# Softmax denominators from spare value columns, keys through DRAM, and one store for eight strips in a four-layer image kernel

## The chip, the core and the metric

The kernel runs on one core of one Trainium2 chip. Its time is the device time of one execution in microseconds; the figure quoted is the median of three runs. In the text PE is TensorE (PEld its weight loads), DVE is VectorE, ACT is ScalarE, POOL is GpSimd and SP is SyncE, which here only issues DMAs.

## The reference, cut to what matters

The input x is 4 images of 16 channels and 512 x 512 pixels. Four layers follow each other.

```python
# layer 0: window attention and MLP (C = 16, 2 heads of 8, windows of 8 x 8 pixels, hidden 64)
x = x + depthwise3x3(x) + pos_b                     # "position"
win = windows(affine(x))                            # 4*64*64 windows of T = 64 tokens
q, k, v = split(win @ qkv_w.T + qkv_b); q = q * 8**-0.5
out = softmax(q @ k.T) @ v                          # per window and head
x = x + out @ proj_w.T + proj_b
x = x + gelu(affine(x) @ fc1_w.T + fc1_b) @ fc2_w.T + fc2_b
# layer 1: fake-quantised 3x3 convolution; mean and variance over the WHOLE image batch; clip to 0..6
# layer 2: conv3x3, relu, conv3x3, + x        layer 3: conv3x3, 1x1 to 128, relu, 1x1 to 16, + x
```

Two facts matter below. The division by the softmax denominator may be done after the product with v. And layer 1 needs the largest |x| and the statistics of its convolution over everything before it can normalise, so the result of layer 0 goes to DRAM (`x1`) and is read back twice.

## The kernel before, in words

All arithmetic is float32 on PE except the quantised convolution of layer 1. There are three stages.

**Layer 0** (`window_attention`) takes 64 steps. The image is cut into 8 horizontal strips of 64 rows; a step does 8 rows and 64 columns of all 8 strips and 4 images at once. Partitions of `y` hold (4 pairs of strips `vv`) x (2 strips of a pair `w`) x 16 channels, its free dimension the 4 images `u` and 512 pixels. Attention wants another order, images on the partition quadrants and window tokens block-diagonal over the two strips; this is the tile `y2`, and `turn_keys` fills it for the next step by 32 small DMAs from `y`, eight at k = 1, 3, 5 and 7.

The order of the work on PE, DVE, ACT and SP is the order in which the source issues it (`manual_schedule`). A step does, for k = 0..7 (one pair of strips, four of its windows):

- `values(k)`: four PE transposes of `y2` into bank 4 or 6, and one DVE copy to `yt`;
- `scores(k)`: 16 matmuls `g` x `y2` into banks 0-3 (the tiles `pair`), then two ACT exponentials of 1024 columns each to `e`. There is one set of these banks, so scores(k+1) waits for both exponentials of k;
- `attend(e, yt, k)`: 16 matmuls of 128 columns, contracting over all 128 partitions (two strips x 64 tokens), give the unnormalised outputs in bank 4 or 6 (line L374); four matmuls of 512 columns with the constant `own` (the right half of tile `hot`) give the denominators, spread over the 16 channels, in bank 5 or 7 (L379);
- `divide(k)`: ACT takes Ln and Exp(-x) of the denominators (L388, L389), DVE multiplies (L390) into `o`.

In the loop scores runs one k ahead of attend and divide. The end of a step does `queries` of the next step (L324, banks 0-3), `project` (L398) with the residual added by DVE (L403), and then a mixed stage in which 16 `hidden` blocks (L411, gelu on ACT L416) are interleaved with the `depthwise` matmuls (L291) of step n + 2. The `output` of a step (fc2, L422, residual L427) is issued at the start of the next step, and every second step `store` writes 8 rows and 128 columns to `x1`: 16 DMAs of 32 KB for each image. The inputs come in by one 2.6 MB load for every two steps (`load`).

Each matmul is recorded twice[...].

**Statistics stage** (start of `conv_layers`): all of `x1` is read in 129 groups of two rows by `_load_pairs`, two DMAs of 256 KB each, into whatever tiles are free; POOL rounds, ACT converts, PE convolves and DVE takes the statistics.

**Layers 1 to 3** (rest of `conv_layers`): 128 iterations; `_load_pairs` reads `x1` a second time (tile `tx`), and between the convolutions SBUF-to-SBUF DMAs shift rows (`zo<-ze`, `ho<-he`, `xo<-xe`, `qo<-qe`).

## Time and profile before

| | us |
|---|---|
| median of 3 runs (6023.52 to 6040.93) | 6026.44 |
| the profiled execution: its time | 6030.1 |
| the profiled execution: its span | 6028.3 |
| of the span: set-up, to the first step | 63.4 |
| layer 0, 64 steps, to 3450 | 3386.6 |
| statistics stage, to 3775 | 325.0 |
| layers 1 to 3, to the end | 2253.3 |

The stage bounds were read off the timeline. A step of layer 0 repeats after 52.67 to 52.70 us in most cases. In the profile's lines "L355 PE MATMUL pair<-g,y 32*128 32x128 f32 x32" means line 355, engine, operation, output tile <- input tiles, the part of the PE array (rows * columns) that one instruction takes, the shape of its moving operand, and how many records are merged. "[1.13 <-ACT e L363]" is the idle time before it and what ended that. In the row of slices each digit is the busy share of one fortieth of the span, in tenths.

### The profile page before, as it was taken

Reading aid. Unit: us, or ns where it says so; the run is one execution under the profiler, and the core shown is the slowest. Engines: PE = TensorE matmul, PEld = TensorE weight load, DVE = VectorE, ACT = ScalarE, POOL = GpSimd, SP = SyncE. Lnnn points to the kernel's source line nnn. Section 1 sums busy time; section 2 is a strip of 40 time slices with the busy share of each in tenths; the row PEclk is TensorE's granted clock in tenths of the full one; section 3 lists DMA queues with packets and bytes.
Section 4 is the critical chain, followed back from the end, with each engine's and each line's share of the span. In section 5 each row is a group of like instructions: output and inputs, shape, how many; then the busy total and the mean of one; then the engine's idle time right before and its main releaser. Section 6 shows DMA issues by size and latency. Waiting matters only on the chain. (4 is left out here: it accounts for less than half of the span.)

```text
span 6028.3 us, 242228 instructions
## 1 busy us (share of the span) xinstructions
PE 5775.3 (96%) x108624; PEld 3084.9 (51%) x108624; DVE 3268.4 (54%) x4648; ACT 3837.6 (64%) x5257; POOL 171.1 (3%) x193
## 2 busy tenths in 40 slices
PE   8999999999999999999999866899999999999999
PEld 5666666666666666666666433333333333333333
DVE  3444444444444444444444455566666666666666
ACT  4777877877787777778777654344444444444444
POOL 0000000000000000000000154000000000000000
PEclk9999999999999999999999999999999999999999
DMA  3233333323333232333333398666676666666663
GB/s 84 58 71 66 64 77 62 78 59 71 67 64 77 61 79 59 71 66 65 77 61 61 58 243 216 163 171 168 167 173 165 168 172 166 168 171 168 167 170 104
DMA packets 638119, 674.57 MB, mean 112 GB/s; under 512 B 371728, under 2 KB 500880, under 8 KB 632976
## 3 DMA queue, kind: packets, MB, share of 16 engines
q1 hardware_dynamic: 635760, 657.53, 47.1%
q8 instruction: 857, 14.04, 1.0%
q0 software_dynamic: 1024, 1.05, 0.1%
q14 instruction: 190, 1.56, 0.1%
q10 hardware_dynamic: 288, 0.39, 0.0%
HBM read 221.15 MB, written 134.48 MB: 59 GB/s over the span
## 5 line engine op out<-in xcount | busy, mean ns | idle before, releaser
L363 ACT ACTIVATE e<-pair 128x1024 f32<-128x1024 f32 x1024 | 992.5, 1021 | 381.7 <-PE pair L355 381.7
L1175 ACT ACTIVATE hid<-tb,vec 128x512 f32<-128x512 f32 x1024 | 620.7, 688 | 517.5 <-PE tb L1167 517.4
L291 PE MATMUL pair<-x,taps 32*32 32x512 f32 x18432 | 927.4, 605 | 2.6 <-ACT y L302 1.2
L1177 DVE TENSOR_SCALAR hid<-tb,vec 128x512 f32<-128x512 f32 x1024 | 695.7, 742 | 2.7 <-PE tb L1167 2.6
L411 PE MATMUL bank<-y,fc_e 32*32 32x512 f32 x8192 | 680.1, 598 | 0.9 <-DVE y L403 0.9
L355 PE MATMUL pair<-g,y 32*128 32x128 f32 x16384 | 653.0, 285 | 26.9 <-ACT y L302 25.0
L355 PEld LDWEIGHTS pair<-g,y 32*128 32x128 f32 x16384 | 542.8, 186 | 215.9 <-issue 108.9
L416 ACT ACTIVATE hid<-bank,f1b 128x512 f32<-128x512 f32 x1024 | 644.5, 686 | 12.4 <-PE bank L411 4.8
L291 PEld LDWEIGHTS pair<-x,taps 32*32 32x32 f32 x18432 | 602.2, 103 | 98.2 <-issue 19.0
L347 DVE COPY yt<-bank 128x512 f32<-128x512 f32 x512 | 347.3, 688 | 540.2 <-PE bank L342 531.9
L1167 PE MATMUL tb<-ye,mat 32*128 32x512 f32 x4096 | 637.6, 624 | 0.3 <-DVE hid L1177 0.3
L374 PE MATMUL bank<-e,yt 128*32 128x128 f32 x16384 | 556.7, 276 | 3.4 <-issue 2.4
L390 DVE TENSOR_TENSOR o<-bank,r 128x512 f32<-128x512 f32 x512 | 354.2, 692 | 372.6 <-ACT r L389 356.3
L379 PE MATMUL bank<-e,hot 128*32 128x512 f32 x4096 | 535.6, 593 | 0.0
L1187 PE MATMUL tb<-hid,mat 128*32 128x512 f32 x4096 | 466.0, 595 | 41.6 <-DVE hid L1177 41.6
L374 PEld LDWEIGHTS bank<-e,yt 128*32 128x32 f32 x16384 | 418.0, 109 | 111.7 <-DVE yt L347 52.8
L306 DVE TENSOR_SCALAR y<-pair,vec 128x512 f32<-128x512 f32 x128 | 90.3, 746 | 706.5 <-PE pair L291 706.5
L1167 PEld LDWEIGHTS tb<-ye,mat 32*128 32x128 f32 x4096 | 267.0, 183 | 323.3 <-issue 219.9
L342 PEld LDWEIGHTS bank<-mat,y 128*128 128x128 f32 x2048 | 216.3, 141 | 376.1 <-issue 270.0
L1092 PE MATMUL tb<-zo,cw 64*32 64x512 f32 x3096 | 362.8, 594 | 14.9 <-issue 8.9
L1092 PE MATMUL tb<-xo,cw 64*32 64x512 f32 x3096 | 366.1, 600 | 10.1 <-issue 7.0
L1092 PE MATMUL tb<-xe,cw 64*32 64x512 f32 x3072 | 361.5, 600 | 0.0
(176 smaller groups left out, 7564.1 us busy)
## 6 DMA issues: line engine op xcount, KB each, us to landing
x<-in_xw_dram SPq DMA_DIRECT2D x32, 2600.0 KB, 10.9
zo<-ze SPq DMA_DIRECT2D x512, 128.5 KB, 2.4
ho<-he SPq DMA_DIRECT2D x512, 128.5 KB, 2.4
xo<-xe SPq DMA_DIRECT2D x512, 128.5 KB, 2.4
y<-y SPq DMA_DIRECT2D x2048, 32.0 KB, 2.2
tx<-x SPq DMA_DIRECT2D x256, 256.0 KB, 4.6
out_dram<-xe SPq DMA_DIRECT2D x128, 512.0 KB, 3.5
x<-xo SPq DMA_DIRECT2D x2016, 32.0 KB, 1.7
```

Source lines behind the costliest of these rows:

```text
L291: nc.tensor.matmul(bank(u)[quad(vv)], taps[quad(u), tap, :], xts[n // 2][quad(u), vv, dy : dy + WS, at : at + BW], start=tap == 0, stop=ta ...
L355: nc.tensor.matmul(bank(u)[:, P * jj : P * jj + P], y2[quad(u), vv, jl + jj].rearrange("p w t -> p (w t)"), g[quad(u), vv, jl + jj].rearra ...
L363: nc.scalar.activation(e[:, 2 * i : 2 * i + 2].rearrange("p u j t -> p u (j t)"), pairs[i], AF.Exp,)
L374: nc.tensor.matmul(b[quad(u), P * jj : P * jj + P], yt[:, jj, quad(u)], e[:, u, jj, :], start=True, stop=True,)
L379: nc.tensor.matmul(d[quad(u)], own, e[:, u].rearrange("p j t -> p (j t)"), start=True, stop=True,)
L411: nc.tensor.matmul(b[quad(k)], fc1[quad(vv), quad(k)], y[quad(vv), u, :], start=True, stop=True,)
L416: nc.scalar.activation(hd, b, AF.Gelu, bias=f1b)
L1092: nc.tensor.matmul(p[r][_quad(2 * f + w)], weights[_half(r), odd, dx, :], src[_half(r), f, dx : dx + W], start=dx == 0, stop=dx == 2,)
L1167: nc.tensor.matmul(p[q], w1[_quad(q), 1 - par, :], inner(src)[_quad(q), f, :], start=True, stop=True,)
L1175: nc.scalar.activation(hd, p[q], AF.Relu, bias=v("l3_b1"))
L1177: nc.vector.tensor_scalar(hd, p[q], v("l3_b1"), 0.0, ALU.add, ALU.max)
L1187: nc.tensor.matmul(p[r][_quad(c)], w2[:, par], hd, start=(r, c) not in seen, stop=(r, c) in seen,)
```

## The change

Layer 0:

- `values` adds a constant `other` instead of copying: the transposed values of a strip have zeros in the 16 columns of the other strip, and these get ones. `attend` then contracts each strip by itself over 64 partitions, so that its 16 output channels and, 16 times over, its denominator come from one matmul of 128 columns. The four matmuls with `own` are gone.
- `empty` copies the two banks to SBUF (`o`, `ts`); `gather` brings one row of denominators of each strip and image to the tile `sums` by two DMAs for each two k; `merge` brings the second strip's outputs from `ts` to their place in `o` by four DMAs.
- One step later, `invert` takes Ln and Exp of `sums` once (two ACT instructions of 1024 columns), and `divide` spreads the inverses by a DVE `stream_shuffle` and multiplies on POOL. Projection, hidden, output and store of a step move one step later, and a 65th pass of the loop finishes the last step. Half of the output moves into the mixed stage.
- `turn_keys` goes through DRAM: `put_keys` writes `y` to `yd` by four DMAs, and eight DMAs read it into `y2` after the step's last scores.
- The input is loaded for each step by itself (1.3 MB), two steps ahead.
- `x1` is laid out as (row pair m in a strip, row r of the pair, strip s, channel, image, column), so that `store` writes all eight strips with one DMA for each r; `_load_pairs` reads this layout.

```diff
-    x1 = dram.tile([H // 2 + 1, 2 * C, B, W], F32, name="x1")
+    x1 = dram.tile([SM, 2, NS + 1, C, B, W], F32, name="x1")     # SM = H // 16
...
+    yd = dram.tile([2, U, 32, V, N], F32, name="yd")
+    sums = [pa.tile([P, 1024], F32, name=f"sums{i}") for i in range(2)]
...
+    def put_keys(n):
+        for u in range(U):
+            nc.sync.dma_start(yd[n % 2, u].rearrange("q v x -> v q x"), ys[n][:, u])
+    def turn_keys(n, i):
+        u, w = divmod(i, 2)
+        at = slice(32 * u + C * w, 32 * u + C * w + C)
+        nc.sync.dma_start(
+            y2[at, :, :, w, :].rearrange("p v j t -> p (v j) t"),
+            yd[n % 2, u, C * w : C * w + C].rearrange("c v (j t) -> c (v j) t", t=T),
+        )
...
-        nc.vector.tensor_copy(t.rearrange("p j c -> p (j c)"), b)
+        nc.vector.tensor_tensor(t..., b..., other.unsqueeze(1).to_broadcast([P, 4 * U, 32]), ALU.add)
...
-        e = px.tile([P, U, 4, P], F32, tag="e", name=f"e{n}_{k}", bufs=3)
+        e = px.tile([P, U, 4, P], F32, tag="e", name=f"e{n}_{k}", bufs=2)
...
     def attend(e, yt, k):
-        b, d = bank(4 + 2 * (k % 2)), bank(5 + 2 * (k % 2))
+        p = bank(4 + 2 * (k % 2)), bank(5 + 2 * (k % 2))
         for jj in range(4):
             for u in range(U):
-                nc.tensor.matmul(
-                    b[quad(u), P * jj : P * jj + P], yt[:, jj, quad(u)], e[:, u, jj, :], ...)
+                for w in range(2):
+                    half = slice(64 * w, 64 * w + 64)
+                    nc.tensor.matmul(
+                        p[w][quad(u), P * jj : P * jj + P],
+                        yt[half, jj, quad(u)], e[half, u, jj, :], ...)
+    def empty(o, k, n):
+        vv, i = divmod(k, 2)
+        if i == 0:
+            ts[vv] = px.tile([P, 1024], F32, tag="t", name=f"t{n}_{vv}")      # 2 buffers
+        nc.vector.tensor_copy(part(o, k), bank(4 + 2 * i))
+        copy = nc.scalar.copy if i else nc.vector.tensor_copy
+        copy(ts[vv][:, 512 * i : 512 * i + 512], bank(5 + 2 * i))
+    def gather(o, vv, n):
+        d = sums[n % 2]
+        nc.sync.dma_start(d[2 * vv : P : 32], pair(o, vv)[C:P:32])
+        nc.sync.dma_start(d[2 * vv + 1 : P : 32], ts[vv][0:P:32])
+    def merge(o, vv):
         for u in range(U):
-            nc.tensor.matmul(d[quad(u)], own, e[:, u].rearrange("p j t -> p (j t)"), ...)
-        nc.scalar.activation(r, d, AF.Ln)
-        nc.scalar.activation(r, r, AF.Exp, scale=-1.0)
-        nc.vector.tensor_tensor(o[:, vv, jl : jl + 4]..., b, r, ALU.mult)
+            at = slice(32 * u + C, 32 * u + 2 * C)
+            nc.sync.dma_start(pair(o, vv)[at], ts[vv][at])
+    def invert(n):
+        d = sums[n % 2]
+        nc.scalar.activation(d, d, AF.Ln)
+        nc.scalar.activation(d, d, AF.Exp, scale=-1.0)
+    def divide(o, k, n):
+        r = px.tile([P, 512], F32, tag="r", name=f"r{n}_{k}")
+        vv, i = divmod(k, 2)
+        nc.vector.stream_shuffle(r, sums[n % 2][:, 512 * i : 512 * i + 512], [2 * vv] * C + [2 * vv + 1] * C)
+        nc.gpsimd.tensor_tensor(part(o, k), part(o, k), r, ALU.mult)
...
# store: one DMA for each r (two where the rows reach into the next strip), partitions = (strip, channel)
+                (next(queues) if k == STEPS // 2 - 1 else nc.sync).dma_start(
+                    x1[mm : mm + rows, r, s : s + 2 * V, :, u, XW * cb : XW * cb + XW].rearrange(
+                        "m s c x -> (s c) m x"),
+                    src[:, at : at + rows])
...
-    for n in range(STEPS):
+    for n in range(STEPS + 1):           # old = the o of step n - 1; done = n - 1
...
         if last:
             output(*last)
+        if old is not None:
+            invert(n - 1)
+            divide(old, 0, n - 1)
         for k in range(1, 8):
...
+                empty(o, k - 1, n)
+                if k % 2 == 0:
+                    gather(o, k // 2 - 1, n)
+                elif k > 1:
+                    merge(o, k // 2 - 1)
+            if old is not None:
+                divide(old, k, n - 1)
# after the loop: queries 0; attend 7, empty 7, gather 3; queries 1, turn_keys(n + 1), merge 3; project(old)
...
-        last = (y, xo, hids, range(U), (5, 7, 4, 6), n)
+                if q == 9:               # in the mixed stage
+                    output(y, xo, hids[:8], (0, 1), (6, 7), done)
+            put_keys(n + 2)
+        if loads:
+            xts[loads] = load(loads)
+        last = (y, xo, hids[8:], (2, 3), (5, 7), done) if old is not None else None
...
 def _load_pairs(nc, t, x1, tt):
+    s, m = divmod(2 * tt, SM)
...
-            t[64 * a : 64 * a + 32 * k],
-            x1[2 * tt : 2 * tt + k, :, 2 * a : 2 * a + 2].rearrange("m c f x -> (m c) f x"),
+            t[64 * a : 64 * a + 32 * k].rearrange("p f x -> p (f x)"),
+            x1[m : m + k, :, s, :, 2 * a : 2 * a + 2].rearrange("m r c f x -> (m r) c (f x)"),
```

## The prediction

> **What bounds the kernel now.** First the page's slices: PE is busy nine tenths everywhere except in slices 24 to 26, and there it is the DMA row that stands at 9 and 8.

> ```profile
> PE   8999999999999999999999866899999999999999
> ...
> DMA  3233333323333232333333398666676666666663
> GB/s 84 58 71 66 64 77 62 78 59 71 67 64 77 61 79 59 71 66 65 77 61 61 58 243 216 163 171 168 167 173 165 168 172 166 168 171 168 167 170 104
> ```

> So layer 0 and layers 1 to 3 are PE's, and the statistics stage is the DMA engines'. Next the timeline of one k in the middle of layer 0:

> ```profile
> 1503.17 1.17 PE L355 MATMUL pair<-g,y 32*128 32x128 f32 x32
> 1504.27 1.08 PE L374 MATMUL bank<-e,yt 128*32 128x128 f32 x32
> 1504.38 1.94 ACT L363 ACTIVATE e<-pair 128x1024 f32<-128x1024 f32 x2 [0.40 <-PE pair L355]
> 1505.17 1.04 PE L379 MATMUL bank<-e,hot 128*32 128x512 f32 x8
> 1506.14 0.66 PE L342 MATMUL bank<-mat,y 128*128 128x128 f32 x4
> 1506.73 1.17 PE L355 MATMUL pair<-g,y 32*128 32x128 f32 x32
> ```

> From start to start PE spends 1.10 us on scores, 0.90 on the products, 0.97 on the denominators, 0.59 on transposes: 3.56 in all, without a gap. But the exponentials end at 1506.32, only 0.41 before the scores that reuse their banks. That is the next limit. The start of layer 0, where nothing else holds PE, shows it bare (a bracket is the idle time and what ended it):

> ```profile
> 67.33 1.94 ACT L363 ACTIVATE e<-pair 128x1024 f32<-128x1024 f32 x2 [0.27 <-PE pair L355]
> 68.40 0.49 PE L355 MATMUL pair<-g,y 32*128 32x128 f32 x4 [0.94 <-ACT e L363]
> 69.32 1.22 PE L355 MATMUL pair<-g,y 32*128 32x128 f32 x28 [0.42 <-ACT e L363]
> 70.36 1.94 ACT L363 ACTIVATE e<-pair 128x1024 f32<-128x1024 f32 x2 [1.10 <-PE pair L355]
> ```

> Scores, exponentials, scores: 70.36 - 67.33 = 3.03 us per k, however little else PE has. Last, the statistics stage: the busy times over a window (PE, PEld, DVE, ACT, POOL, then clock, DMA share, GB/s) and the wait before POOL's rounding.

> ```profile
> 3455.00:3760.00 305.00, 197.05 (x3100) 108.26 (x3100) 183.08 (x285) 154.47 (x136) 145.51 (x141) 0.94 0.96 231
> ```
> ```profile
> 3605.81 1.12 POOL L980 TENSOR_SCALAR xo<-xo,inv_x 128x1024 f32<-128x1024 f32 x1 [0.97 <-DMA xo<-x]
> 3607.85 1.12 POOL L980 TENSOR_SCALAR xo<-xo,inv_x 128x1024 f32<-128x1024 f32 x1 [0.92 <-DMA xo<-x]
> ```

> No compute engine passes 65%, the DMA engines are at 96%, each group waits for its load. 231 GB/s over 16 engines at 0.96 is 15.0 GB/s each, 0.272 us per packet of 4 KB.

> [...] starts lie 7 ns apart in L374, and in layers 1 to 3 eight tiles of 64*32 do 512 columns every 0.43 us:

> ```profile
> 5200.18 0.61 PE L1092 MATMUL tb<-zo,cw 64*32 64x512 f32 x4
> ...
> 5200.61 0.61 PE L1092 MATMUL tb<-zo,cw 64*32 64x512 f32 x4
> ```

> [...]

> **The change part by part.** *Attend.* The denominators' 0.97 us goes. 64 records of 64*32 instead of 32 of 128*32: eight pairs fill a round of 128 columns; a round takes 0.109 us now (the L374 records), eight starts 7 ns apart take 0.056, so eight rounds take some 1.03. PE then has 1.10 + 1.03 + 0.59 = 2.72 per k, and the 3.03 of the scores-exponential ring sets the pace. If the tiles did not run abreast, attend would take some 1.8 and k 3.5: that end costs 64 x 8 x 0.45 = 230 us. I take 1.03.

> *ACT and DVE in the loop.* ACT loses Ln and Exp (0.60 + 0.63) and gains a 0.6 copy every second k: 1.94 + 0.6 fits in 3.03. DVE: add for yt 0.69 (as the copy L347), one or two bank copies of 0.69, one shuffle[...]

> *One step* (52.68 before). From its start to the exponential of k = 2 it is 1553.36 - 1542.39 = 10.97; half of fc2 (3.64 / 2) leaves, invert puts two ACT instructions of about 1.0 before exponential 1: some 9.97, gain 1.0. Five more k: 17.97 before (3.73 + 4 x 3.56), 15.15 after: gain 2.8. After k = 7 the chain exponential, queries, bank copies on DVE and ACT, queries remains; the wait for the last divide goes, but two more copies stand in the queue: gain 0.15. In the mixed stage 416 records at 34 ns are PE-bound over 14.1 us; half of fc2 with two array-mode changes adds 2.05. Net: 1.9 less, 50.8.

> *Queues.* SP issues 64.5 DMAs of 0.59 us in a step now, 41 after, so issuing is no bound. But put_keys has an outermost size of 4 on the DRAM side: [...] a merge overwrites rows that its gather reads, so SP waits there, and the next gather is behind it. `ts` has two buffers, so empty(4) waits for merge(0): my count has it due at 22 us of the step and landing at 22.5 to 23 or, with stores, 27. DVE then holds up yt and PE by 1 to 5 us: 3 on average at worst, nothing if the landings are quicker. I take half. turn_keys has some 18 us from the last scores to the next values and is covered.

> Layer 0 in sum: 64 x (1.5 - 1.9) = -26; the first pass has no hidden and no output, -11; the extra pass (invert, 8 shuffles and products, project, 16 gelus, output) +29; the first keys through DRAM start after both positions instead of one, +10. Sum +2, from -95 without stalls to +100 with all of them.

> *Statistics stage.* The new source of a load is (row pair, row) = 4, then 16 channels of 4 KB. [...] 258 DMAs of 64 packets are 16,512; now 1032 on each of 16 engines x 0.272 = 281 us; after, 4128 on each of four. With twelve engines silent a packet should take the least that the trace's packet records show for 4 KB, 0.16 us (5th percentile of `tx` loads): 660 us, **+380**. At the 0.22 of the median tx packet it is +627. [...]

> *Layers 1 to 3.* An iteration of 17.34 us has DMA engines busy 0.69 of it, 12 us. [...] the transfers queued behind (qo, xo) are needed 9 us or more later: +10. At the upper end up to +200.

> Stores: the same packets in fewer DMAs; nothing, being covered by a 50 us step; at the end some us less, within the sum's error.

> Sum against the profiled 6030.1: + 2 + 380 + 10 = 6422; the median of the runs stands 3.7 lower. I say 6420.

> **Rivals.** A, above: 0.77. B, slower packets [...]: 6030 + 2 + 627 + 100 = 6760; for it, 0.16 is only the fastest twentieth; against it, those ran among fifteen busy neighbours: 0.10. C, the loads still run on 16 engines, since the pattern that is issued may be reshaped: then the stage keeps its 281 us and layer 0 decides; without stalls 6030 - 95 = 5935, faster. The point from which it decides is the number of engines: 16,512 x 0.16 / E = 281 + 95 gives E = 7. For it: fewer PE cycles where PE is the bound[...]: 0.09. D, 16 engines, but SP's chain of gathers and merges stalls DVE: 6130: 0.04. That attend does not run abreast would add 230 to any of these; it lies inside the range of A.

> **How the numbers follow.** 0.3% (18 us) is about what a measurement here can tell from no change. Slower: A, B and D, 0.91, less 0.02 for the middle between C and D, so 0.89; same 0.02; faster 0.09. The range takes A with layer 0 at its best and B's centre: 6270 to 6780.

> **What would show it.** xe<-x landing in well over its 8.5 us; a DMA share near 0.25 in a statistics stage of some 700 us; no L379, k at 3.0 us with scores waiting for ACT; DVE waiting for DMA in some steps. A statistics stage of 325 us would make the forecast wrong.

## The result, and the profile after

| | before | after |
|---|---|---|
| median, us (range) | 6027.88 (6023.52 to 6040.93) | 6742.44 (6720.82 to 6770.38) |
| profiled execution, us | 6030.1 | 6770.38 |
| its span, us | 6028.3 | 6768.6 |

The changed kernel is slower: ratio 1.1184, 95 % interval 1.1137 to 1.1231. The forecast was 6420 us with a range of 6270 to 6780.

The spans differ by 740.3 us. Cut at the same places in both traces (first value transpose, start of step 63, first and last matmul of the statistics):

| stretch | before | after | difference | forecast |
|---|---|---|---|---|
| set-up, to step 0 | 63.4 | 90.0 | +26.6 | +10 |
| 63 steps of layer 0 | 3323.6 | 3621.2 | +297.6 | about -37 |
| last step, extra pass, first loads | 73.9 | 113.2 | +39.3 | +29 |
| statistics stage | 280.4 | 646.6 | +366.2 | +380 |
| layers 1 to 3 | 2287.0 | 2297.6 | +10.6 | +10 |

Four rows came out within 17 us of what was worked out beforehand, and one did not. The slices of the page show both places. They are the busy tenths of one fortieth of the span each:

```profile
PE   6888888888889888888889544459999999999999
...
PEclk8999999999999999999999666669999999999999
DMA  3555555555555555555555222246666666666664
GB/s 92 95 106 101 97 99 103 104 103 104 94 105 101 108 97 108 98 108 98 94 100 94 68 105 105 105 121 167 168 168 169 169 168 168 169 168 168 168 170 111
```

PE stands at 8 instead of 9 nearly all through layer 0, and the DMA row there has gone from 2 and 3 to 5. In the slices of the statistics stage 9 and 8 have become 2, at a flat 105 GB/s where there were 243 and 216.

*The statistics stage.* A window over it (busy times of PE, PEld, DVE, ACT and POOL, then clock, DMA share, GB/s), and the wait before POOL's rounding:

```profile
3830.00:4440.00 610.00, 294.64 (x2900) 139.86 (x2896) 158.60 (x244) 139.24 (x121) 137.19 (x131) 0.65 0.26 105
```
```profile
4104.99 1.12 POOL L1066 TENSOR_SCALAR zo<-zo,inv_x 128x1024 f32<-128x1024 f32 x1 [4.39 <-DMA zo<-x]
4110.01 1.12 POOL L1066 TENSOR_SCALAR ye<-ye,inv_x 128x1024 f32<-128x1024 f32 x1 [3.90 <-DMA ye<-x]
```

A group comes every 5.0 us instead of 2.2, and POOL waits some four of these for the load. The DMA share is 0.26: of 16 engines 4.2 are at work, on average. Their 4 KB packets take 0.161 us.

*The loop of layer 0*, in a stretch with nothing in its way:

```profile
2013.39 1.94 ACT L378 ACTIVATE e<-pair 128x1024 f32<-128x1024 f32 x2 [1.13 <-PE pair L370]
2013.40 1.16 PE L391 MATMUL bank<-e,yt 64*32 64x128 f32 x64
...
2016.46 1.94 ACT L378 ACTIVATE e<-pair 128x1024 f32<-128x1024 f32 x2 [0.65 <-PE pair L370]
2016.47 1.16 PE L391 MATMUL bank<-e,yt 64*32 64x128 f32 x64
```

The 64 records of attend run abreast (starts 7 ns apart, the median of L391), 1.16 us together, and a k takes 2016.46 - 2013.39 = 3.07 us: the ring of scores and exponentials. At other places it looks like this:

```profile
2024.41 0.69 DVE L411 COPY t<-bank 128x512 f32<-128x512 f32 x1 [4.87 <-DMA o<-t]
...
2026.37 1.96 PE L391 MATMUL bank<-e,yt 64*32 64x128 f32 x64 [3.69 <-DVE yt L358]
```

DVE may not write `ts` before `merge` has read it. It waits 4.87 us for that DMA, `yt` behind it is late, and PE waits for `yt`. DVE's wait in the whole run (total us, times, longest):

```profile
DVE t L411 <- DMA o<-t: 129.0, 57, 5.7
```

In 34 cases PE then waited for `yt`, 72.5 us in all.

*The mixed stage* (hidden blocks and depthwise matmuls) is where most of the loss lies. Its windows, first one step of the kernel before, then three steps of the changed kernel (columns as above):

```profile
736.58:750.56 13.98, 13.98 (x442) 11.32 (x417) 2.72 (x4) 13.05 (x19) 0.00 (x0) 1.00 0.32 50
```
```profile
1159.27:1178.67 19.40, 17.63 (x450) 8.66 (x432) 8.55 (x9) 13.14 (x19) 0.00 (x0) 1.00 1.04 123
1970.83:1996.36 25.53, 21.41 (x461) 9.96 (x444) 8.56 (x9) 12.62 (x19) 0.00 (x0) 0.80 0.74 86
2089.40:2105.43 16.03, 16.03 (x451) 10.40 (x432) 8.55 (x9) 12.77 (x19) 0.00 (x0) 1.00 1.06 148
```

The stage took 14 us in every step before. After, it takes 16.03 at best and 20.1 on average. In the second of the three the granted clock is 0.80 on average: it is 0.5 for 10.24 us, from 1980.53 to 1990.77. Such spells, at a granted clock of 0.5, are called half speed below. In the first the clock is full and PE is idle for 1.8 us. And the DMA share is 0.7 to 1.1 where it was 0.1 to 0.3. What stops PE in the first of them:

```profile
1164.02 0.77 PE L297 MATMUL pair<-x,taps 32*32 32x512 f32 x4
1166.50 0.63 PE L297 MATMUL pair<-x,taps 32*32 32x512 f32 x4 [1.72 <-issue]
```

"Issue" means that PE waited for nothing that the profile shows as a wait: no buffer, no other engine. Half of the experiments are about this stop.

### The profile page after: what moved, and what is told of

The parts are those of the page before. It is cut to its first block, busy times and chain, and to the rows that moved or that the text cites. A ratio compares the mean times of both kernels' runs of the same rounds, so it can differ in the third digit from the quotient of the medians.

```text
span 6768.6 us, 268191 instructions
## 1 busy us (share of the span) xinstructions
PE 5828.0 (86%) x120912; PEld 3065.9 (45%) x120912; DVE 3725.6 (55%) x5928; ACT 3488.0 (52%) x4619; POOL 811.5 (12%) x681
## 5 line engine op out<-in xcount | busy, mean ns | idle before, releaser
L437 POOL TENSOR_TENSOR o<-o,r 128x512 f32<-128x512 f32 x512 | 650.7, 1271 | 3099.8 <-DVE r L433 2904.2
L391 PE MATMUL bank<-e,yt 64*32 64x128 f32 x32768 | 632.3, 280 | 91.1 <-DVE yt L358 72.5
L297 PEld LDWEIGHTS pair<-x,taps 32*32 32x32 f32 x18432 | 480.4, 104 | 344.1 <-issue 235.9
L1103 PE MATMUL tb<-qe,cq 64*64 64x512 bf16 x3072 | 312.7, 562 | 354.1 <-ACT qe L1069 354.1
L358 DVE TENSOR_TENSOR yt<-bank,hot 128x512 f32<-128x512 f32 x512 | 346.7, 687 | 458.4 <-PE bank L353 456.5
L391 PEld LDWEIGHTS bank<-e,yt 64*32 64x32 f32 x32768 | 476.9, 108 | 225.5 <-DVE yt L358 117.1
L477 DVE TENSOR_TENSOR xo<-bank,y 128x512 f32<-128x512 f32 x256 | 177.1, 692 | 504.5 <-PE bank L472 266.4
L1109 DVE BATCH_NORM_STATS2 stats<-tb 128x6 f32<-128x512 f32 x256 | 165.8, 690 | 477.1 <-PE tb L1103 477.1
L1103 PEld LDWEIGHTS <-cq 64*64 64x64 bf16 x3072 | 148.3, 146 | 518.5 <-issue 495.6
L433 DVE STREAM_SHUFFLE r<-sums 128x512 f32<-128x512 f32 x512 | 375.3, 733 | 0.9 <-issue 0.4
```

The lines of the kernel that those rows point to most:

```text
L297: nc.tensor.matmul(bank(u)[quad(vv)], taps[quad(u), tap, :], xts[n][quad(u), vv, dy : dy + WS, dx : dx + BW], start=tap == 0, stop=tap == 8,)
L391: nc.tensor.matmul(p[w][quad(u), P * jj : P * jj + P], yt[half, jj, quad(u)], e[half, u, jj, :], start=True, stop=True,)
L437: nc.gpsimd.tensor_tensor(b, b, r, ALU.mult)
```

## The experiments

Step times below are means over steps 2 to 59 of the profiled run, good to about 0.1 us. The stages of a step, in us (even and odd steps, since every second step stores); the last column is explained under "What the traces showed at this point":

| kernel | step | five k periods, k = 3 to 7 | k = 7 to depthwise | mixed stage | us at half speed, a step | fetch stops in the mixed stage, us a step |
|---|---|---|---|---|---|---|
| before | 52.8 | 18.0 / 18.2 | 9.2 / 9.2 | 14.0 / 14.0 | 0 | 0 |
| after | 57.8 | 15.9 / 17.4 | 9.9 / 11.5 | 20.5 / 19.6 | 4.9 | 2.8 |
| after, step 34 | 51.0 | 15.3 | 9.3 | 16.0 | 0 | 0 |
| e3 | 56.9 | 15.7 / 17.2 | 9.6 / 11.3 | 19.6 / 19.7 | 3.8 | 2.5 |
| e4 | 57.1 | 16.7 / 18.6 | 9.3 / 9.4 | 19.6 / 19.8 | 3.2 | 2.7 |
| e5 | 56.9 | 15.7 / 15.7 | 13.5 / 14.9 | 16.7 / 16.6 | 5.8 | 0 |
| e6 | 55.5 | 15.7 / 17.5 | 9.6 / 11.4 | 18.1 / 17.8 | 3.1 | 1.4 |
| e8 | 57.1 | 15.7 / 17.5 | 9.6 / 11.4 | 19.8 / 19.6 | 4.1 | 2.4 |
| e9 | 52.5 | 15.8 / 17.3 | 9.3 / 9.5 | 16.0 / 16.2 | 0.6 | 0 |
| e11 | 55.1 | 15.7 / 16.4 | 9.3 / 9.4 | 19.7 / 19.1 | 1.7 | 2.6 |
| e2 | 53.5 | 18.0 / 18.0 | 9.2 / 9.2 | 15.7 / 14.0 | 0 | 0.8 |
| e10 | 53.5 | 18.0 / 18.3 | 9.2 / 9.2 | 14.7 / 14.8 | 0 | 0.5 |
| e12 | 59.8 | 18.0 / 18.2 | 9.2 / 9.2 | 17.4 / 16.6 | 6.1 | 2.7 |

### e1 and e2: the layout of x1, undone alone and done alone

e1 puts the old layout into the changed kernel; a store becomes one DMA for each row:

```diff
-    x1 = dram.tile([SM, 2, NS + 1, C, B, W], F32, name="x1")
+    x1 = dram.tile([H // 2 + 1, 2 * C, B, W], F32, name="x1")
...
+        for row in range(WS):
+            r, m = 1 - row % 2, WS // 2 * i + (row + 1) // 2
+            nc.sync.dma_start(
+                x1[m : m + SM * (NS - 1) + 1 : SM, C * r : C * r + C, u, XW * cb : XW * cb + XW],
+                xo[:, u, row],
+            )
```

> The changed kernel with the x1 of the kernel before: row pairs outermost, the 32 (row, channel) lines of a pair one behind the other, so that the loads of both later stages again have one outermost size of 64 in memory; the store of layer 0 becomes one DMA for each of 8 rows, 64 KB over all eight strips (32 in two steps instead of 8). Theory 1 (the loads run on 4 DMA engines): the distance of two groups in the statistics stage falls from 5.05 us to 2.1 or less, the stage from about 670 us to about 325, layers 1 to 3 lose some 15 us, layer 0 stays at about 3740 us although SP issues 12 DMAs more in a step; time 6742 - 360 = 6380 us. Rival (the stage is slow because of something else that the new layout did, such as rows far apart in DRAM, or the fetches are late for want of buffers): the distance stays near 5 us and the time at 6740.

6631.05 us (ratio to before 1.1019, 1.0995 to 1.1043). The stage did what theory 1 says and more. Its window and POOL's waits:

```profile
4060.00:4300.00 240.00, 180.97 (x2908) 100.26 (x2910) 158.50 (x244) 140.43 (x123) 139.88 (x134) 0.99 1.03 270
```
```profile
4102.47 1.12 POOL L1054 TENSOR_SCALAR xe<-xe,inv_x 128x1024 f32<-128x1024 f32 x1 [0.91 <-DMA xe<-x]
4104.54 1.12 POOL L1054 TENSOR_SCALAR xe<-xe,inv_x 128x1024 f32<-128x1024 f32 x1 [0.95 <-DMA xe<-x]
```

Share 1.03, 270 GB/s, a group every 2.0 us: 257 us from the first to the last matmul of the stage instead of 647. "Layer 0 stays" was wrong. The row stores have an outermost size of 8 in memory, and I had looked at that size only for the loads. The odd steps grew to 67.7 us, with k = 7 alone at 13.0, where DVE waits for `ts` and PE for DVE. On the page:

```profile
L388 PE MATMUL bank<-e,yt 64*32 64x128 f32 x32768 | 641.1, 285 | 368.6 <-DVE yt L355 343.3
```

That is 343 us against 72.5 in the changed kernel. That the outermost size of the stores is the reason was not shown: the records carry no engine numbers.

e2 is the reverse: the kernel before with only the new layout, its stores and its loads.

> The kernel before with one part of the change alone: the new layout of x1, the stores for all strips at once, and the loads that read it. Theory 1: layer 0 keeps its step of 52.7 us (the stores were hidden and are hidden), the statistics stage grows from 325 to about 670 us, layers 1 to 3 by 15; time 6028 + 360 = 6390 us. Rival (56 DMAs fewer in two steps relieve SP and the DMA engines): the step of layer 0 falls by 0.5 us or more and the time is under 6360. Other rival (the new stores take part in the slow layer 0): the step grows to 54 or more, the time is over 6470.

6451.6 us (1.0714, 1.0696 to 1.0732). The statistics stage took 647.9 us, +367.5, as in the changed kernel: the layout alone does it. But 41 us came from layer 0, where nothing was expected. Its even steps grew from 52.7 to 54.4, all in the mixed stage (15.7); in even steps the stores of the step before go out. And the stop looks like the one above:

```profile
749.27 0.63 PE L295 MATMUL pair<-x,taps 32*32 32x512 f32 x4 [1.14 <-issue]
```

### e3: the hidden buffers

My first suspect for the mixed stage was a cut in the diff that the prediction had passed over: `hid` has 8 buffers instead of 16, so gelu 8 waits for fc2.

```diff
-        hd = px.tile([P, N], F32, tag="hid", name=f"hid{n}_{u}_{vv}", bufs=8)
+        hd = px.tile([P, N], F32, tag="hid", name=f"hid{n}_{u}_{vv}", bufs=10)
```

> The changed kernel with 10 instead of 8 buffers for the hidden blocks: the gelus of hidden 8 and 9 then need not wait for fc2 of hidden 0 and 1, which PE does only behind the matmuls of hidden 9. Theory 2 (that wait opens the gap in the mixed stage, and the gap lets PE's clock be halved): ACT's idle time of about 3 us in front of gelu 8 goes, the mixed stage falls from 20 us to 16 to 17.5, the step from 57.8 to 54.5 to 55.5; time 6742 - 63 x 2.3 to 3.3 = 6535 to 6600 us. Rival (half speed of the clock comes from the stops in the loop over k, and the wait of gelu 8 only fills time in which PE has depthwise work): the mixed stage stays over 19 us, the time within 40 us of 6742.

6728.4 us (1.1171, 1.1147 to 1.1194): its interval overlaps that of the changed kernel. ACT's wait for fc2, 169.4 us in the changed kernel, is gone, and the mixed stage still takes 19.7. Theory 2 fell. The 0.9 us by which the step got shorter says nothing: e8, which leaves layer 0 as it is in the changed kernel, has 57.1 us too.

### e4: put_keys as sixteen DMAs

```diff
-            nc.sync.dma_start(
-                yd[n % 2, u].rearrange("q v x -> v q x"), ys[n][:, u]
-            )
+            for vv in range(V):
+                nc.sync.dma_start(yd[n % 2, u, :, vv], ys[n][quad(vv), u])
```

> The changed kernel with put_keys as 16 DMAs of 32 partitions each instead of 4 whose outermost size is 4: the same bytes, [...] 12 DMAs more for SP in a step. Theory 3 (the gathers and merges are late [...]): DVE's wait for the DMA that empties ts (129 us in the whole run) falls under 40 us, the k periods of 4 to 7 us in the loop go, and with them the half speed that follows them; time 6742 - 64 x 1.5 to 3.5 = 6520 to 6650 us. Rival (they are late because of the load of 1.3 MB, the stores, or SP itself, which stands at a merge until its gather is done): the wait stays above 80 us and the time within 40 us of 6742, or above it for the 7 us more that SP issues.

6728.15 us (1.1161, 1.1133 to 1.1189). Theory 3, that the gathers and merges come late because of `put_keys`, was half right; by which engines the two meet was my assumption, and no record shows it. DVE's wait for `ts`, 129 us in the changed kernel, is now 4.1 us, and k = 7 to depthwise is back at 9.3. But the time did not follow: k = 4 and 5 now take 3.5 to 5.0 us, again with stops of PE that no wait explains (ahead of the attend matmuls 62 us in the run, where the changed kernel has 17.6). Of these, 38 of the 39 over 0.3 us are of the kind that the next section finds.

### What the traces showed at this point

The DMA records of the trace hold packets of 16 KB in a queue that no line of the kernel issues. The page lists it, before and after:

```profile
q8 instruction: 857, 14.04, 1.0%
```
```profile
q8 instruction: 950, 15.56, 1.0%
```

The time after a fetch could be chance; the place in the program can't. Number PE's records (matmuls, weight loads and semaphore waits) in order of time, and subtract 256, the instructions of one block, for every fetch that has ended. In the mixed stages of steps 2 to 59 the changed kernel has 61 stops over 1 us, and at the end of each of the 61 the rest is 192 or 193. So it is at all the others over 1 us in these stages, 25 in e2, 36 in e6, 14 in e10 and 52 in e12, and 489 in the ten runs that have any; each ends 1.2 to 2.4 us after the end of a fetch. The kernel before, e5, e7 and e9 have none. A constant rest says that PE has run to the end of what was fetched and goes on with the next block: it waits for its instructions. The last column of the table sums the stops over 0.53 us with this rest.

The count also tells how far ahead the fetches run. In layer 0 of the kernel before, a fetch begins 226 instructions before its first one is due (the median; 307 at most) and has ended 169 before. So PE has about one block in hand, some 4 us at 17 ns each, and stops when a fetch comes later than that.

### e5 and e6: the keys as before, and half of the keys

e5 undoes the keys alone: `put_keys` and `yd` go, and `turn_keys(ys[n + 1], k // 2)` is back at k = 1, 3, 5 and 7.

> The changed kernel with the keys of the kernel before: no put_keys, no tile in DRAM; turn_keys fills y2 straight from y by 32 DMAs, eight at each of k = 1, 3, 5 and 7. So the 4096 pieces of 256 bytes that the key transfer makes in a step are spread over the loop and no longer stand in the mixed stage. Theory 4, formed from the traces of the runs so far (PE's instructions are themselves fetched by DMA, 16 KB at a time; in the mixed stage these fetches take 1.51 us on average instead of 1.10 and up to 2.2, and 3.1 of the 5.2 us of stops of PE in it end 1.2 to 2.4 us after the end of a fetch: PE waits there for its own instructions, behind the key transfers): the mixed stage falls from 20 to 16.2 to 17 us, half-speed windows in it go, the step from 57.8 to 51.5 to 53.5, the time to 6742 - 64 x 4.3 to 6.3 = 6340 to 6470 us. Rival (the stops belong to the mixed stage itself, the fc2 blocks and table loads in it): the mixed stage stays above 18.5 and the step above 56. Second rival (SP with 61 DMAs in a step, and the gathers behind the key DMAs, make the loop slower by as much): mixed stage short, but k periods of 4 us or more and a step of 55 to 58.

e6 leaves everything in place and issues four of the eight DMAs:

```diff
-            for i in range(2 * U):
+            for i in range(U):
                 turn_keys(n + 1, i)
```

> The changed kernel with only the first four of the eight DMAs of turn_keys in every step: the keys and values of images 2 and 3 keep what they had in step 0, so their attention is computed from old data (this part of the computation is left out); every other instruction is as in the changed kernel. Theory 4: half of the 4096 pieces are gone from the mixed stage, its fetches come sooner; the mixed stage falls from 20 to between 16.5 and 18.5, the step to 54.5 to 56.5, the time to 6540 to 6660. Rival (stops of the mixed stage itself): mixed stage above 19, time within 40 us of 6742.

e5 took 6711.69 us (1.1143, 1.1112 to 1.1174), e6 6619.1 (1.0986, 1.0955 to 1.1016), which is where theory 4 had it. The mixed stage follows the traffic: 20.1 with all keys in it, 18.0 with half, 16.65 with none; so do the fetch stops, 2.8, 1.4 and 0 us a step. Two steps of e5:

```profile
1353.83:1370.64 16.81, 16.81 (x463) 10.17 (x445) 8.55 (x9) 12.32 (x19) 0.00 (x0) 0.99 0.50 97
1411.87:1428.50 16.63, 16.63 (x463) 10.15 (x431) 8.55 (x9) 12.11 (x18) 0.00 (x0) 0.99 0.29 46
```

PE is busy through the whole window, and the stops of every kind fell from 5.2 us a step to 1.1, as in the undisturbed step (3.1 in e6). In e5 the time was nevertheless lost again, as its second rival had it, only at a different place than I put it: eight key DMAs now stand in SP's queue ahead of each gather and merge, so the last copy waits for `ts`:

```profile
1291.84 0.69 DVE L405 COPY t<-bank 128x512 f32<-128x512 f32 x1 [4.13 <-DMA o<-t]
```
```profile
DVE t L405 <- DMA o<-t: 224.5, 65, 7.0
```

The queries' results stand behind that copy on DVE. k = 7 to depthwise grew from 10.7 to 14.2 us on average, PE stood still for 5.6 us in the step shown, and half speed came in every step (5.8 us a step).

### e7, e10 and e12: traffic added to the kernel before

These three leave the kernel before as it is and add DMAs that nothing waits for. e7 adds eight like those of `turn_keys`, DRAM to DRAM, on SP.

> The kernel before with an addition only: after the last queries of every step SP issues eight DMAs of 128 KB, each in pieces of 256 bytes, from one tile in DRAM to another that nothing reads, in the place where the changed kernel has turn_keys. No engine waits for them. Theory 4: PE is stopped in the mixed stage for its own instructions, this stage grows from 14.0 to 15.5 to 18 us, with stops that end 1.2 to 2.4 us after a fetch; time 6028 + 64 x 1.5 to 4 = 6120 to 6280. Rival (DMA traffic that nobody waits for is free, as the kernel before has slack on SP and on the DMA engines): 6028 within 25 us.

6024.96 us (0.9994, 0.9981 to 1.0007): nothing. It did not test what it was meant to. SP is so far behind in that kernel that the new DMAs went out half in the next loop, and the DMA engines stood at 31 (even) and 38 % in the mixed stage, against 31 and 13. It shows that this much of this kind is free. e10 therefore takes POOL's queue and waits for the new `y`:

```diff
         project(y)
+        for u in range(U):
+            nc.gpsimd.dma_start(
+                y3[:, u, :, 0], y[:, u].rearrange("p (j t) -> p j t", t=T)
+            )
```

> The kernel before with an addition only: after project of each step POOL issues four DMAs of 256 KB from the new y to a tile in DRAM that nothing reads, in 4096 pieces of 256 bytes; they start when DVE has written y, at the start of the mixed stage, and do not stand behind SP's other DMAs as those of e7 did (e7 left the DMA engines 29 to 37 % busy in the mixed stage, the changed kernel 79 to 94 %). Theory 4: with the DMA engines over 70 % busy in the mixed stage PE stops there for its own instructions; the stage grows from 14.0 to 15.5 to 19 us; time 6028 + 64 x 1.5 to 5 = 6120 to 6350. Rival (the stops in the changed kernel come from its own order of work, and DMA traffic alone does nothing): mixed stage below 14.5, time 6028 within 25 us.

6067.98 us (1.0071, 1.0050 to 1.0092). The sign is theory 4's, the size below both its bounds and outside the rival's. The packets were not the 256 bytes that I had written but 4096, and the share rose to 57 (even) and 48 % only. e12 has the same three times over.

> As e10, but three DMAs instead of one for each of the four parts of y, to three places: 3 MB more in every step of the kernel before, again from POOL at the start of the mixed stage and read by nothing. e10 showed that POOL's DMAs go out in packets of 4096 bytes rather than 256, some 256 a step of about 0.29 us, which brought the DMA engines to 46 to 55 % in the mixed stage, and gave 0.7 us of growth there and 0.5 us of stops a step, all ending 1.2 to 1.6 us after a fetch. Theory 4 (PE waits for its own instructions when the DMA engines are full): three times as many, 768 x 0.29 / 16 = 14 us, fill the mixed stage; it grows from 14.0 to 15.5 to 19 us, mostly by stops after fetches, and the clock is halved in some steps as in the changed kernel; time 6028 + 64 x 1.5 to 5 = 6120 to 6350. Rival (e10's 0.7 us was the price of something else, such as POOL's or the memory's traffic beside DVE and ACT, and the stops of the changed kernel come from its own order of work): growth at most three times 0.7 without stops after fetches, or none beyond e10: 6030 to 6100.

6466.07 us (1.0731, 1.0710 to 1.0752), above the 6120 to 6350 expected. With the engines over 80 % busy the kernel before shows the disease of the changed one: stops of 3.0 us a step in the mixed stage, 2.9 of them ending 1.2 to 2.4 us after a fetch, and half speed (6.1 us a step) where it had none. Two mixed stages, and one stop:

```profile
814.70:835.33 20.63, 16.13 (x442) 10.93 (x417) 3.37 (x5) 13.27 (x19) 10.53 (x12) 0.88 0.81 172
995.11:1013.01 17.90, 15.12 (x441) 9.19 (x417) 2.73 (x4) 13.21 (x19) 10.53 (x12) 0.95 0.87 168
```
```profile
826.19 1.80 PE L293 MATMUL pair<-x,taps 32*32 32x512 f32 x33
832.50 2.02 PE L293 MATMUL pair<-x,taps 32*32 32x512 f32 x32 [4.50 <-issue]
```

The fetch before this stop ended at 821.7. The next, due some 4 us later at that pace, began only at 830.2 and ended at 831.1; PE went on at 832.5. The order of PE's work was untouched, so neither fc2 in the mixed stage nor the buffers are needed for the effect: traffic is enough. The step grew by 7.0 us, the mixed stage by 3.0; most of the rest lies behind it, where PE waits for keys that are now late too (`DMA y<-y`, 152.9 us in the run, 2.4 a step). Only the 3.0 are evidence for theory 4.

### e8, e9, e11: repairs

e8 gives the loads an outermost size of 16 within the new layout, as eight DMAs a group on three queues.

```diff
+        for q in range(2 * k):
+            at = 64 * a + C * q
+            queue = nc.sync if not first or q < 2 else (nc.scalar, nc.gpsimd)[q % 2]
+            queue.dma_start(t[at : at + C], x1[m + q // 2, q % 2, s, :, 2 * a : 2 * a + 2])
```

> The changed kernel with its layout of x1 and its stores, but the loads of both later stages as one DMA of 64 KB for each row and image pair, with an outermost size of 16: eight DMAs a group instead of two; in the statistics stage SP issues four of them, ACT two and POOL two, in layers 1 to 3 SP all eight. Theory 1: [...] the groups come every 2.1 to 2.8 us (SP's four issues take 2.2 us, POOL's two and its rounding 2.7), the stage falls from about 650 to 280 to 370 us; layer 0 unchanged; time 6742 - 280 to 370 = 6370 to 6460. Rival (issuing eight DMAs a group on three queues costs what the engines gain, or ACT and POOL stop at them): the stage stays above 450 us.

6544.28 us (1.0865, 1.0825 to 1.0905). The stage took 436 us, 3.65 us a group once the first 19 were used up: better by 210, where 280 to 370 us had been expected for the whole stage. It is no longer the DMA engines (share 0.70) but POOL, which waits for ACT before it issues:

```profile
4104.95 1.02 POOL L999 DMA_DIRECT2D xe<-x  x2 [1.48 <-ACT qe L1070]
4106.00 1.12 POOL L1067 TENSOR_SCALAR xe<-xe,inv_x 128x1024 f32<-128x1024 f32 x1
4108.60 1.02 POOL L999 DMA_DIRECT2D xe<-x  x2 [1.48 <-ACT qe L1070]
```

e11 has three buffers `ts` instead of two and nothing else.

> The changed kernel with three instead of two buffers ts and nothing else. Theory 3: DVE's wait for the DMA that empties ts (129 us in the whole run) falls under 20, the k periods over 4 us in the loop go, so do the stops after the loop; gain 64 x 1.5 to 2.5 us, with the half speed that follows these stops up to 3.5; time 6742 - 100 to 220 = 6520 to 6640. Rival (the waits are only moved: the mixed stage, starved of instructions, takes 20 us as before and half speed comes from there): the loop gets shorter by less than 1 us in a step, the time is within 60 us of 6742.

6613.87 us (1.0977, 1.0947 to 1.1008), within the expectation. k = 7 to depthwise is back at 9.3 and half speed falls from 4.9 to 1.7 us a step, but the mixed stage stays at 19.4 and the fetch stops at 2.6 us. So the late merges and the late instructions are two causes: e11 removes the first without the second, e5 the second without the first.

e9 combines the keys of before, three `ts`, and the loads of e8 issued two groups later.

> The changed kernel with three parts altered: the keys as in the kernel before (as in e5); three instead of two buffers ts, so that the copy of k = 6 need not wait for the merge of k = 3 behind the key DMAs; the loads as eight DMAs of outermost size 16 (as in e8), in the statistics stage issued two groups later into the same buffers, so that POOL's issue no longer waits for ACT's conversion of the group before. If all three theories hold (1: loads on 4 engines; 3: gathers and merges late; 4: PE waiting for its instructions behind the key transfers): mixed stage 16.2 to 17, from k = 7 to the depthwise matmuls 9.2 to 10 instead of 13.5 to 15 in e5, nearly no half speed, step 51.2 to 52.3; statistics stage 285 to 330 us; time 5930 to 6030, at or below the kernel before. Rival (half speed and stops come from the attend and merge scheme itself, whatever the keys do): step 54 or more, time above 6120.

6243.31 us (1.0360, 1.0342 to 1.0379), above the 6030 hoped for. Layer 0 came close to what was expected: mixed stage 16.1, step 52.5 for 51.2 to 52.3, and over 63 steps 3299.3 us, 24 below the kernel before.

```profile
1253.70:1269.69 15.99, 15.99 (x450) 10.41 (x432) 8.55 (x9) 12.76 (x19) 0.00 (x0) 1.00 0.35 55
1306.72:1322.74 16.02, 16.02 (x452) 10.61 (x432) 8.55 (x9) 12.79 (x19) 0.00 (x0) 1.00 0.35 54
```

The rest is the loads: the statistics stage still has 3.66 us a group (+152 us against before), so issuing two groups later did not free POOL, and what its DMAs wait for in ACT stays open; and with the extra pass and the first loads, now 19 tiles of eight DMAs on SP, ACT and POOL, the way from the last step to the statistics is 80 us longer than before. No run beat the kernel before. Of the parts measured here, layer 0 at its best wins 24 us and the last step with the extra pass costs 39 in the changed kernel, so that repaired loads alone would not bring a gain; that is an estimate, not a run.

## Why the prediction was right and wrong

- **Loads on four engines: right.** Packet 0.16 us forecast, 0.161 measured; stage +380 against +366. e2 shows it alone, e1 takes it away alone. Rival C falls. That it is four engines rests on the share, 0.26 of 16; the records name no engine. That the outermost size of 4 would bring it about was my assumption, and the main forecast rested on it: every transfer of the kernel before has an outermost size that 16 divides. Measured here: a share of 0.26 with 4, 1.03 with 64 (e1), 0.70 with 16 (e8, where POOL is the limit).
- **Layers 1 to 3, +10: right** (+10.6; +9.3 in e2, with the layout alone). It was an estimate under the same assumption: of the `tx` packets of an iteration, 8 of 0.22 us on each of 16 engines become 32 of 0.16 to 0.22 on each of four, so that these are busy 15.4 to 17.3 us of 17.34.
- **Attend, right:** abreast, 1.16 us against 1.03, and the ring sets 3.07 against 3.03. DVE, ACT and POOL have room: from 2010.30 to 2019.50, three k, they are busy 6.58, 6.29 and 3.81 of 9.20 us. No trace of before shows a shuffle or a product on POOL; they take 0.73 and 1.27 us.
- **Queues: right in mechanism, small in size.** 1 to 5 us of stops by late merges were forecast, 3 on average at worst, and 1.5 taken. SP stood at merges for a gather to land, 262.1 us in the run (193 times). e11 prices the stop with the half speed that follows it at 57.8 - 55.1 = 2.7 us, or 2.0 against e8's 57.1. e4 shows the source: with `put_keys` in 16 DMAs the wait for `ts` is 4.1 us in the run instead of 129.0.
- **One step: the term that failed is the mixed stage, "+2.05".** That is what the work costs: 16.03 - 13.98 in the one step that nothing disturbed, which took 50.96 us where 50.8 stood in the text. (In that step the change of the array's form into fc2 takes 0.52 us from the last record to the next, as does the one out of it, where rounds of four records within fc2 follow each other in 0.41 to 0.43.) The mean is +6.1. The missing 4.0 us a step are some 250 of the 348 us by which the profiled execution lies above the sum of 6422; most of the rest is the queue item, which shows at the end of the step, and the set-up. I wrote of the moved `turn_keys` that it "has some 18 us ... and is covered". It lands in time. What I did not ask is whom it delays while it is on its way: PE's instruction fetch. The sum has no term for it. 2.8 of the 4.0 us are fetch stops; half speed inside the stage lasts 2.3 us a step and, if it costs half of that, makes up 1.1 more, an estimate.
- **End of a step, "-0.15":** +1.5 on average, since the wait for `ts` reaches into it; without that wait (e11) it is +0.1.
- **Set-up and extra pass:** +10 and +29 forecast, +27 and +39 measured. The set-up is the first keys through DRAM, for which PE waits 28.2 us; in e5, without them, it takes 62.0.
- **Rival B** (6760) stands nearer to the result than the forecast and is nevertheless wrong: its 627 us in the statistics stage were 366, its 100 in layers 1 to 3 were 11.
- **That 6742 lies inside the range is luck.** The upper end, 6780, came from B's slow packets. Layer 0 with set-up and extra pass was put at +2, with +100 as the worst; it cost some 363 us.

What stays open: what starts half speed. The spells here last 3.41 us or a multiple, but for one of 4.61 at the very end of the run. No stop of PE as long as one spell need stand before them: 65 begin in layer 0 of the changed kernel, and for 52 of them the longest stop of PE in the 7.5 us before is under 3.41 us (the median of the 65 is 2.5). Half speed is no condition for the fetch stops: e2 and e10 have them without any. By e11 some 2 to 3 of the 4.9 us at half speed belong to the late merges; the rest was not divided further. Full DMA engines also don't delay every fetch: the undisturbed step above had a share of 1.06. And a mean share is no threshold: even steps of e2 lose 1.7 us at 0.45, while even steps of e5 have no fetch stop at 0.49.

## What to carry to other kernels

When DMAs are moved or merged, ask not only whether they land in time but what shares the engines with them; here PE, with an instruction every 16 to 18 ns in the mixed stage, needs a 16 KB fetch every 4 to 5 us, and heavy traffic made that fetch late (2.8 us of stops a step in the changed kernel, 2.7 in e12). Idle time that the profile puts down to "issue", in a window with much DMA traffic, is a hint of it; the proof here were stops that always end at the same place of a block of 256 instructions (61 of 61). And look at the outermost size, in DRAM, of every DMA that a new layout touches: loads with 4 there came every 5.0 us a group, with 64 every 2.0 (e1), and beside row stores with 8 PE's waits for `yt` came to 343 us instead of 72.5 (e1).

## What the runs showed that I had not expected

- PE's instruction fetch can be a bound: 3 MB of unread traffic a step brought the kernel before 2.7 us of fetch stops in each mixed stage of 14 us. (Its 7.3 % are more than that: keys came late too.)
- All 489 stops over 1 us in the mixed stages of all runs end at the same place of a block of 256 instructions, and PE has about one block in hand.
- Such traffic on the kernel before cost nothing at DMA shares of 31 and 38 % in the mixed stage, 0.7 us a step at 48 and 57 %, and 3 us in that stage alone at over 80 %.
- POOL's DMAs went out in packets of 4096 bytes where the pattern has runs of 256.
- A ring of POOL's own DMA issue (1.02 us for two), its rounding (1.12) and a wait for ACT (1.48) set 3.65 us a group in e8.
